# Maxima's steps as one sequence over all units, four or eight steps ahead

## The chip, the cores and the metric

The kernel runs on one core of a Trainium2 chip. The metric is device time in microseconds (us), the median of three runs: 1900.68 us, between 1898.97 and 1903.65. One further execution was profiled; its own time was 1904.93 us, and the profile's span, from the first to the last of the program's own instructions, is 1903.1 us.

Names of engines: TensorE (PE in the profile; PEld are its weight loads), VectorE (DVE), ScalarE (ACT), GpSimd (POOL) and SyncE (SP), which here issues DMAs only. All engines work through their own list of instructions in the order in which the kernel wrote them, and wait for each other by semaphores.

## The reference

The reference has four layers over x, 2048 tokens of 256 features in float32:

```python
x = x + attn_a(layernorm(x))   # 16 query heads, 4 key heads, head size 16, rotary, biases, causal
x = x + ffn(layernorm(x))      # gate and up 256 -> 2048, tanh-gelu, down 2048 -> 256, 4-bit weights
x = x + attn_b(layernorm(x))   # 16 query heads, 16 key heads, causal
x = x + ffn(layernorm(x))      # the same weights
```

In both attentions a row of probabilities is the softmax of q·k/4 over all earlier keys, and the result is the sum of values weighted by it. Only the two attentions are touched by the change.

## The kernel before

**Tiling.** The tokens are cut into four blocks b of 512, and the heads into four groups g of four. One pass of `Attention.run` (L837) goes through 16 units (b, g) in order; the kernel makes two passes, one for each attention. For a unit, softmax is computed in two sweeps over the causal triangle.

The first sweep finds each query's maximum. `scores(i, c, p)` (L651) takes 128 queries i, one block of keys c and one pair of heads p: two matmuls (L658) into a PSUM buffer `ps_s` with queries on partitions, and one VectorE reduce over the keys (L670) into `mx`. A unit of block b has 8(b+1) such steps. On the diagonal block of keys (c equal to b) only the first 128(i+1) keys are computed, and a causal mask is added by eight small matmuls (L633) before the reduce. `gather` (L679) reduces `mx` over the blocks of keys and splits the negated maximum into three bf16 parts, in five small VectorE operations (L682 to L692) that write `m_pad`. `turn` (L696) turns `m_pad` by four matmuls (L699) so that queries stand along the free dimension, and ScalarE copies the result to `mT` (L705).

The second sweep computes the weighted values. `pair(kt, p)` (L739) takes 128 keys kt and a pair of heads p: two matmuls with `sel` put the negated maxima from `mT` into a `ps_s` buffer (L747), two add the scores, this time with keys on partitions (L752), a diagonal pair gets its mask (L633), and ScalarE takes the exponential into `e` (L764). `values` (L718) multiplies `e` by the values into `ps_av` (L732), one block of keys behind the pairs. A unit has 8(b+1) pairs. `end` (L775) does the last values and copies `ps_av` to `o` on ScalarE (L779); `divide` (L782), which runs early in the following unit, turns `o` (L786) and divides by the sums on VectorE (L791, L794).

**What sets the order.** Everything is written out by hand, one step after another, for all engines. `weave(main, side, rest=2)` (L42) puts side steps between main steps in even shares, so that the side steps are used up two main steps before the end. `blend(a, b)` (L60) merges two lists in proportion. In a unit the main steps are its pairs and values. The side steps are the divide of the unit before, and a blend of the maxima's steps of the following unit with other work: preparation of the next block (projections, rotary, the round trip of q and k through DRAM: L426 to L620), output projection of the block before (L806), and in the first pass the unpacking of the feed-forward weights (L307). After the weave come the turn of the following unit's maxima, and then `end`. The very first unit's maxima and turn stand outside of the loop (L978, L994).

**Masks that are owed.** The mask of a diagonal pair or score is not issued at once: it is put on the list `owed`, and the next step calls `settle` (L638) to issue it with the exponential or the reduce behind it. Pairs, values and `gather` settle everything. A score settles only where a score's mask is owed.

**Buffers.** PSUM holds three `ps_s` of two banks each, used in rotation by pairs and scores, one `ps_av` and one `ps_m`. The turn uses `ps_m`, as do divide, preparation and output projection. `qT` has three buffers: at the start of unit n, `load_q` (L610) issues eight DMAs on SP for unit n+2. `mT` and `mx` have two buffers, `m_pad` one.

Of the kernel before, what the change touches and what calls it, by code (L numbers as in the profile page):

```python
# [26 lines left out]
NG = NH // 4  # L27
# [14 lines left out]
def weave(main, side, rest=0):  # L42


    done = 0
    for n, step in enumerate(main):
        first, *second = step if isinstance(step, tuple) else (step,)
        first()
        want = min(len(side), -(-(n + 1) * len(side) // max(1, len(main) - rest)))
        while done < want:  # L50
            side[done]()
            done += 1
        for f in second:
            f()
    while done < len(side):
        side[done]()
        done += 1


def blend(a, b):  # L60

    keyed = [((n + 0.5) / len(a), 0, n, f) for n, f in enumerate(a)]
    keyed += [((n + 0.5) / len(b), 1, n, f) for n, f in enumerate(b)]
    return [f for *_, f in sorted(keyed, key=lambda k: k[:3])]
# [3 lines left out]
def tile_hybrid_layers(  # L68
# [40 lines left out]
    def ps_s():  # L109
        return psum.tile([P, 2, 512], F32, tag="s", name="ps_s", bufs=3)  # L110
# [4 lines left out]
    def ps_m():  # L115
        return psum.tile([P, 512], F32, tag="m", name="ps_m")
# [36 lines left out]
    for src, at in ((bq, 0), (bk, D), (bv, D + 64)):  # L153
        n = src.shape[1]
# [240 lines left out]
    class Attention:  # L395
# [11 lines left out]
        def __init__(self, first, wqkv):  # L407
            self.first, self.wqkv = first, wqkv
            self.kvh = NKV if first else NH
            self.npair = NKV if first else NH // 2  # L410
            self.krows = self.kvh * HD
            self.kT, self.vv, self.qT, self.mT, self.att = {}, {}, {}, {}, {}
            self.q_d, self.k_d = {}, {}
            self.owed = []

        def place(self, pool, b):

# [220 lines left out]
        def settle(self, kind=None):  # L638


            due = [f for k, f in self.owed if kind in (None, k)]
            if due:
                due, self.owed = self.owed, []
                for _, f in due:
                    f()

        def max_steps(self, b, g):

            held = {}

            def scores(i, c, p):  # L651
                if not held:
                    held["mx"] = self.wk.tile([P, NT, 4, NB], F32, tag="mx", name="mx")
                w = TB if c < b else (i + 1) * P
                self.settle("max")
                pt = ps_s()
                for r in range(2):
                    nc.tensor.matmul(  # L658
                        pt[:, r, :w],
                        lhsT=self.qT[b, g][64 * r : 64 * r + 64, p, i * P : (i + 1) * P],  # L660
                        rhs=self.key_rows(c, g, p, r, slice(0, w)),
                        start=True, stop=(c < b),
                    )

                def masked():
                    self.add_mask(pt, 0, w - P)
                    reduced()

                def reduced():
                    nc.vector.tensor_reduce(  # L670
                        held["mx"][:, i, 2 * p : 2 * p + 2, c], pt[:, :, :w], AX.X, ALU.max
                    )

                if c == b:
                    self.owed.append(("max", masked))
                else:
                    reduced()

            def gather():  # L679
                self.settle()  # L680
                nm = self.wk.tile([P, NT, 4], F32, tag="nm", name="nm")
                nc.vector.tensor_reduce(  # L682
                    nm, held["mx"][:, :, :, : b + 1], AX.X, ALU.max, negate=True
                )

                to = m_pad[:, :, :, :6].rearrange("q t r (p s) -> q t p r s", s=3)
                rest = nm.rearrange("q t (p r) -> q t p r", r=2)
                nc.vector.tensor_copy(to[:, :, :, :, 0], rest)
                less = self.wk.tile([P, NT, 2, 2], F32, tag="rest", name="rest")
                nc.vector.tensor_tensor(less, rest, to[:, :, :, :, 0], ALU.subtract)  # L690
                nc.vector.tensor_copy(to[:, :, :, :, 1], less)
                nc.vector.tensor_tensor(  # L692
                    to[:, :, :, :, 2], less, to[:, :, :, :, 1], ALU.subtract
                )

            def turn():  # L696
                pt = ps_m()
                for i in range(NT):
                    nc.tensor.matmul(  # L699
                        pt[:, i * P : (i + 1) * P],  # L700
                        lhsT=m_pad[:, i].rearrange("p r c -> p (r c)"), rhs=ident_b,
                        start=True, stop=True,
                    )
                self.mT[b, g] = self.wk.tile([P, TB], BF16, tag="mT", name="mT")
                nc.scalar.copy(self.mT[b, g], pt)  # L705

            steps = [
                lambda i=i, c=c, p=p: scores(i, c, p)
                for i in range(NT) for c in range(b + 1) for p in range(2)
            ]  # L710
            return steps + [gather], turn
# [125 lines left out]
        def run(self, extra, beside):  # L837


            units = [(b, g) for b in range(NB) for g in range(NG)]  # L840
            per_unit = -(-len(extra) // (len(units) - NG))
            late, ahead = [], []
            for n, (b, g) in enumerate(units):
                more = []
                if g == 0 and b > 0:
                    more += self.out_steps(b - 1)
                if g == 0 and b + 1 < NB:
                    ahead = self.prep_steps(b + 1)
                    few = -(-len(ahead) // 2)
                if n >= NG:  # L850
                    more, extra = more + extra[:per_unit], extra[per_unit:]
                if g < 2:
                    more, ahead = more + ahead[:few], ahead[few:]
                if n + 2 < len(units):
                    self.load_q(*units[n + 2])
                steps, turn = [], None
                if n + 1 < len(units):
                    steps, turn = self.max_steps(*units[n + 1])
                else:
                    more += beside  # L860
                side = late + (blend(steps, more) if steps else more)
                steps, end, divide = self.value_steps(b, g)
                weave(steps, side, rest=2)
                if turn:
                    turn()
                end()
                late = [divide]
            return late + [lambda: None] * 2 + self.out_steps(NB - 1)
# [93 lines left out]
    with tc.tile_pool(name="wk1", bufs=2) as wk, tc.tile_pool(name="kv1", bufs=1) as kv:  # L962
        at.wk = at.qpool = wk
        with tc.tile_pool(name="init", bufs=1) as pool:
# [13 lines left out]
            steps, turn = at.max_steps(0, 0)  # L978
# [6 lines left out]
    with tc.tile_pool(name="kv20", bufs=1, reuse_waits="tile") as kv0, tc.tile_pool(  # L985
# [8 lines left out]
        steps, turn = at.max_steps(0, 0)  # L994
# [60 lines left out]
```

## Time and profile before

| what | value |
|---|---|
| median of three runs | 1900.68 us |
| profiled execution, its own time | 1904.93 us |
| span of the profile | 1903.1 us |
| TensorE busy | 1772.5 us, 93% |
| VectorE busy | 1121.3 us, 59% |
| ScalarE busy | 812.9 us, 43% |
| GpSimd busy | 239.0 us, 13% |
| first pass of attention, units | 51 to 651 us |
| second pass of attention, units | 1011 to 1558 us |

A group of instructions is told in one row: source line, engine, operation, what it writes and reads, how often; then after the first bar its busy time in us and the mean of one in ns; after the second bar the idle time of the engine just before these instructions, and who ended that idle time. Matmuls are pipelined and their ends are modelled, so a busy TensorE is not TensorE at its peak. A row of the timeline has the start in us from the span's start, the length in us, the engine, the line and what is done; in brackets the idle time of that engine before it and who ended it. In the busy time by stretch, the columns are the stretch, its length, and for each engine its busy time and the count of instructions; then the granted clock of TensorE, the DMA engines' share and what they moved.

### The profile page before, as it was taken

To read this page: it belongs to the slowest core of one execution; us is meant where nothing else is said; L and a number is where in the kernel's file an instruction comes from. 1 tells how busy PE (TensorE), PEld (TensorE's weight loads), DVE (VectorE), ACT (ScalarE), POOL (GpSimd) and SP (SyncE) were. 2 spreads that over 40 slices of the span, in tenths; PEclk is the share of its full clock that TensorE was granted. 3 is DMA by queue.
4 is the path that set the end of the run, shared out by engine and by line. 5 is a ranking of instruction groups with operands and counts; after the bars stand their busy time and mean duration, and the time that the engine had idled before them with its cause. 6 is when DMAs were issued, how large, how long until landed. Compare 5 with 4: busy or idle time off the path is not lost. (4 is left out here: it accounts for less than half of the span.)

```text
span 1903.1 us, 31836 instructions
## 1 busy us (share of the span) xinstructions
PE 1772.5 (93%) x13452; PEld 930.8 (49%) x13452; DVE 1121.3 (59%) x1676; ACT 812.9 (43%) x1069; POOL 239.0 (13%) x437
## 2 busy tenths in 40 slices
PE   5788889998999999999998899999899999999999
PEld 3344444344444446566555444444444444756656
DVE  4466587678788153535345667767877715363442
ACT  1334345465666631312223455555566663131221
POOL 4211311310010010111212010010000001011110
PEclk8879899999999999999999899999999999999999
DMA  4511310310101100000403241050000010000000
GB/s 105 118 46 34 73 26 26 72 41 24 34 24 35 45 6 1 0 1 20 102 1 80 56 83 41 12 95 19 23 7 7 2 46 1 11 1 11 7 6 12
DMA packets 42271, 64.24 MB, mean 34 GB/s; under 512 B 13840, under 2 KB 20880, under 8 KB 41872
## 3 DMA queue, kind: packets, MB, share of 16 engines
q1 hardware_dynamic: 33488, 45.93, 8.3%
q0 software_dynamic: 7680, 15.74, 5.0%
q8 instruction: 106, 1.74, 0.4%
q10 hardware_dynamic: 960, 0.52, 0.1%
q14 instruction: 37, 0.30, 0.1%
HBM read 44.24 MB, written 17.83 MB: 33 GB/s over the span
## 5 line engine op out<-in xcount | busy, mean ns | idle before, releaser
L764 ACT ACTIVATE e<-ps_s 128x1024 f32<-128x1024 f32 (+3 forms) x640 | 573.4, 897 | 433.7 <-PE ps_s L752 216.5
L670 DVE TENSOR_REDUCE mx<-ps_s 128x2 f32<-128x1024 f32 (+3 forms) x640 | 656.8, 1060 | 160.9 <-PE ps_s L633 93.2
L732 PE MATMUL ps_av<-e,v 128*32 128x256 f32 (+1 forms) x4608 | 370.6, 386 | 0.7 <-ACT e L764 0.7
L752 PE MATMUL ps_s<-qT,kT 64*128 64x512 f32 (+3 forms) x1280 | 341.9, 527 | 0.0
L658 PE MATMUL ps_s<-kT,qT 64*128 64x512 f32 (+3 forms) x1280 | 268.6, 428 | 45.4 <-DVE mx L670 20.1
L747 PE MATMUL ps_s<-mT,sel 64*128 64x512 bf16 (+3 forms) x1280 | 232.6, 357 | 36.7 <-DVE mx L670 21.4
L915 PE MATMUL ps_s<-xnT,wg 128*128 128x512 f32 x512 | 240.8, 593 | 0.0
L915 PE MATMUL ps_s<-xnT,wu 128*128 128x512 f32 x512 | 240.6, 592 | 0.0
L747 PEld LDWEIGHTS <-sel 64*128 64x128 bf16 x1280 | 77.1, 93 | 275.8 <-issue 269.4
L658 PEld LDWEIGHTS ps_s<-kT,qT 64*128 64x128 f32 x1280 | 125.7, 191 | 150.9 <-ACT e L764 66.9
L923 DVE TENSOR_TENSOR t<-ps_s,t 128x512 f32<-128x512 f32 x128 | 88.1, 689 | 166.4 <-POOL t L922 164.5
L921 ACT ACTIVATE t<-ps_s 128x512 f32<-128x512 f32 x128 | 76.2, 596 | 246.7 <-PE ps_s L915 246.3
L924 ACT ACTIVATE t<-t 128x512 f32<-128x512 f32 x128 | 80.6, 629 | 201.0 <-DVE t L923 201.0
L915 PEld LDWEIGHTS ps_s<-xnT,wu 128*128 128x128 f32 x512 | 97.3, 190 | 122.5 <-issue 122.5
L922 POOL TENSOR_SCALAR t<-t 128x512 f32<-128x512 f32 x128 | 79.3, 620 | 571.1 <-ACT t L921 570.6
L732 PEld LDWEIGHTS ps_av<-e,v 128*32 128x32 f32 x4608 | 97.0, 109 | 102.8 <-issue 79.8
L915 PEld LDWEIGHTS ps_s<-xnT,wg 128*128 128x128 f32 x512 | 95.3, 190 | 105.2 <-issue 103.5
L925 DVE SCALAR_TENSOR_TENSOR t<-t,ps_s 128x512 f32<-128x512 f32 x128 | 88.0, 688 | 89.0 <-ACT t L924 89.0
L752 PEld LDWEIGHTS ps_s<-qT,kT 64*128 64x128 f32 x1280 | 130.4, 198 | 0.0
L940 PE MATMUL ps_m<-wd,inter 128*128 128x256 f32 x512 | 114.5, 380 | 0.0
L940 PE MATMUL ps_av<-wd,inter 128*128 128x256 f32 x512 | 114.5, 380 | 0.0
L633 PE MATMUL ps_s<-mask_t,mask_w 64*128 64x64 bf16 x2048 | 108.4, 199 | 0.0
(125 smaller groups left out, 1171.5 us busy)
## 6 DMA issues: line engine op xcount, KB each, us to landing
qT<-h SPq DMA_DIRECT2D x256, 64.0 KB, 2.2
kT<-h POOLq DMA_DIRECT2D x96, 128.0 KB, 5.7
h<-high SPq DMA_DIRECT2D x24, 256.0 KB, 3.3
h<-low SPq DMA_DIRECT2D x24, 256.0 KB, 3.0
wd<-wd_kept SPq DMA_DIRECT2D x2, 2048.0 KB, 7.8
wd_kept<-dq_d SPq DMA_DIRECT2D x4, 512.0 KB, 2.7
out<-x SPq DMA_DIRECT2D x16, 128.0 KB, 1.7
x<-x SPq DMA_DIRECT2D x3, 512.0 KB, 5.2
```

What stands on the lines that cost most here:

```text
L633: nc.tensor.matmul(pt[:, r, to], lhsT=mask_w[rows, kind, part, :], rhs=mask_t[rows, kind, part, :], start=False, stop=(part == 1),)
L658: nc.tensor.matmul(pt[:, r, :w], lhsT=self.qT[b, g][64 * r : 64 * r + 64, p, i * P : (i + 1) * P], rhs=self.key_rows(c, g, p, r, slice(0, w)),
L670: nc.vector.tensor_reduce(held["mx"][:, i, 2 * p : 2 * p + 2, c], pt[:, :, :w], AX.X, ALU.max)
L732: nc.tensor.matmul(held["av"][32 * j : 32 * j + 32, own], lhsT=self.vv[kt // NT][:, kt % NT, h * VW : h * VW + 32], rhs=es_[j // 2][:, j % ...
L747: nc.tensor.matmul(pt[:, r, q0:], lhsT=sel[64 * r : 64 * r + 64, p, :], rhs=self.mT[b, g][64 * r : 64 * r + 64, q0:], start=True, stop=False,)
L752: nc.tensor.matmul(pt[:, r, q0:], lhsT=self.key_rows(kt // NT, g, p, r, keys), rhs=self.qT[b, g][64 * r : 64 * r + 64, p, q0:], start=Fals ...
L764: nc.scalar.activation(e[:, :, q0:], pt[:, :, q0:], AF.Exp, scale=QK_SCALE)
L915: nc.tensor.matmul(pt[:, k, :], lhsT=w[:, c, fc * P : (fc + 1) * P], rhs=self.xnT[b][:, c, :], start=(c == 0), stop=(c == 1),)
L923: nc.vector.tensor_tensor(t, gate, t, ALU.mult)
L924: nc.scalar.activation(t, t, AF.Tanh, scale=GELU_C)
L925: nc.vector.scalar_tensor_tensor(t, t, 1.0, gate, ALU.add, ALU.mult)
L940: nc.tensor.matmul(po[:, :D], lhsT=inter[:, fc, i * P : (i + 1) * P], rhs=wd[:, fc, :], start=(fc == 0), stop=(fc == NFC - 1),)
```

## The change

Before, a unit carries exactly the maxima's steps of the following unit, and the turn stands at its end. After, the maxima's steps of all units form one sequence, and a unit carries what is left of the following unit's steps and the first four of the unit after that; in the third unit of a block, the first eight (which belong to the next block). The first unit of a pass takes none ahead. The turn is put into this sequence two early steps after the gather, it takes a `ps_s` buffer in place of `ps_m`, and settles what is owed first. In the last unit but one the turn follows the gather after one empty step. `settle` counts scores in a row: the first after another step behaves as before, and from the second on everything owed is settled. The scores, pairs, values, reduces, exponentials and DMAs are the same in number and shape.

```diff
@@ settle
-            due = [f for k, f in self.owed if kind in (None, k)]
-            if due:
+            self.row = self.row + 1 if kind else 0
+            if self.row != 1 or kind in [k for k, _ in self.owed]:
                 due, self.owed = self.owed, []
                 for _, f in due:
                     f()
@@ max_steps
             def turn():
-                pt = ps_m()
+                self.settle()
+                pt = ps_s()[:, 0, :]
                 for i in range(NT):
                     nc.tensor.matmul(
@@ run
             late, ahead = [], []
+
+            due, turn = self.max_steps(*units[1])
             for n, (b, g) in enumerate(units):
...
                 if n + 2 < len(units):
                     self.load_q(*units[n + 2])
-                steps, turn = [], None
-                if n + 1 < len(units):
-                    steps, turn = self.max_steps(*units[n + 1])
+                steps = due
+                if n + 2 < len(units):
+                    coming, next_turn = self.max_steps(*units[n + 2])
+                    early = 0 if n == 0 else 8 if g == NG - 2 else 4
+                    steps, due = due + coming[:early], coming[early:]
+                    steps.insert(len(steps) - max(early - 2, 0), turn)
+                    turn = next_turn
+                elif n + 1 < len(units):
+                    steps, due = due + [lambda: None, turn], []
                 else:
                     more += beside
                 side = late + (blend(steps, more) if steps else more)
                 steps, end, divide = self.value_steps(b, g)
                 weave(steps, side, rest=2)
-                if turn:
-                    turn()
                 end()
                 late = [divide]
```

More of the change, by code (lines that the diff above doesn't have):

```diff
@@ L413, in __init__ @@
             self.q_d, self.k_d = {}, {}
-            self.owed = []
+            self.owed, self.row = [], 0
         def place(self, pool, b):
```

## The prediction

> **What bounds the kernel.** I read the page's busy times first (TensorE 93%, VectorE 59%), then TensorE's groups for what ended its idle time, then busy time unit by unit (a unit is one block of 512 queries and one group of four heads), then the timeline across a unit's end. TensorE's groups that the change touches:
>
> ```profile
> L658 PE MATMUL ps_s<-kT,qT 64*128 64x512 f32 (+3 forms) x1280 | 268.6, 428 | 45.4 <-DVE mx L670 20.1 <-ACT e L764 12.9 <-DMA qT<-h 10.2
> L747 PE MATMUL ps_s<-mT,sel 64*128 64x512 bf16 (+3 forms) x1280 | 232.6, 357 | 36.7 <-DVE mx L670 21.4 <-ACT mT L705 4.8 <-ACT e L764 4.4
> L699 PE MATMUL ps_m<-ident_b,m_pad 128*128 128x128 bf16 x128 | 13.3, 229 | 11.0 <-DVE m_pad L692 8.9 <-DVE low L541 1.6 <-DVE x L946 0.5
> ```
>
> The last columns are TensorE's idle time ahead of the group and its releasers. The turn (L699) waits 11.0 us in all, the pairs behind it 4.8 us for mT, and scores and pairs 41.5 us for VectorE's reduces, which hold the ring of three ps_s buffers.
>
> Busy time by unit in the first pass: units (0,2), (0,3), (2,2), (2,3), (3,1):
>
> ```profile
> core 0: us, PE busy (x) PEld busy (x) DVE busy (x) ACT busy (x) POOL busy (x), PEclk, DMA share, GB/s
> 104.70:117.80 13.10, 11.55 (x171) 6.35 (x171) 7.86 (x15) 6.88 (x11) 0.00 (x0) 0.96 0.14 42
> 117.80:141.10 23.30, 20.25 (x188) 10.72 (x187) 17.25 (x23) 6.58 (x11) 0.00 (x0) 0.63 0.07 23
> 385.80:421.20 35.40, 33.87 (x394) 16.03 (x395) 28.83 (x39) 23.08 (x27) 4.43 (x9) 1.00 0.09 30
> 421.20:464.90 43.70, 37.46 (x411) 17.38 (x411) 37.63 (x47) 23.26 (x27) 4.63 (x9) 1.00 0.10 28
> 517.10:564.30 47.20, 45.41 (x508) 20.51 (x508) 38.55 (x47) 31.35 (x35) 4.58 (x9) 1.00 0.13 41
> ```
>
> A block's fourth unit computes the next block's maxima, eight scores more than its pairs. There VectorE is as busy as TensorE (37.6 against 37.5 of 43.7 us), and TensorE idles 6.2 us; in the third unit it idles 1.5. Unit (3,1) has 96% TensorE: it is bound by TensorE.
>
> The timeline from the end of (3,1) into (3,2), where the turn waits for nothing, and one row from the end of (1,3), where it does:
>
> ```profile
> 563.00 0.23 PE L633 MATMUL ps_s<-mask_t,mask_w 64*128 64x64 bf16 x4
> 563.17 0.40 PE L699 MATMUL ps_m<-ident_b,m_pad 128*128 128x128 bf16 x4
> 563.34 0.38 ACT L764 ACTIVATE e<-ps_s 128x256 f32<-128x256 f32 x1 [0.54 <-PE ps_s L633]
> 563.50 0.69 PE L732 MATMUL ps_av<-e,v 128*32 128x128 f32 x8
> 563.62 0.58 ACT L705 CAST mT<-ps_m 128x512 bf16<-128x512 f32 x1
> 564.23 0.59 ACT L779 COPY o<-ps_av 128x512 f32<-128x512 f32 x1
> 564.25 0.39 PE L747 MATMUL ps_s<-mT,sel 64*128 64x512 bf16 x2
> 564.87 0.65 PE L786 MATMUL ps_m<-ident,o 128*128 128x128 f32 x4
> 565.57 0.26 DVE L791 RECIPROCAL rec<-ps_m 128x16 f32<-128x16 f32 x1 [2.46 <-PE ps_m L786]
> 567.47 0.39 PE L747 MATMUL ps_s<-mT,sel 64*128 64x512 bf16 x2 [0.82 <-DVE mx L670]
> ...
> 285.88 0.40 PE L699 MATMUL ps_m<-ident_b,m_pad 128*128 128x128 bf16 x4 [0.98 <-DVE m_pad L692]
> ```
>
> The turn stands in the shadow of another chain: the last exponential ends at 563.72, the values that need it follow, then o (564.82), the divide's transposes (564.87), rec and att, the first reduce, and the third pair's wait of 0.82 us. The turn and mT fit beside that.
>
> **What the Trainium skill says.** "TensorE: Matmul & The Clock Gate", section Step-by-step, keeps matmuls in program order and lets only weight loads go ahead. The trace agrees: ready values stood 0.98 us behind the turn at 285.88. Its Part 1 says that TensorE's clock is throttled by default and released by activity; (0,3), the unit with the longest VectorE waits for its size, shows a granted clock of 0.63. "PSUM — Partial Sum Buffer", Specifications, gives eight banks of 2 KiB: three ps_s of two banks, av and m fill them, so the turn's new buffer must come out of that ring; no run shows the count of banks. "Perfetto Trace Analysis", section Identifying the Most-Contended Engine, warns that busy matmuls are no measure of headroom; I use idle time before matmuls instead.
>
> **The change, part by part.** The sum is against the profiled execution (span 1903.1, its own time 1904.93 us); the difference is carried to the median of the three runs, 1900.68.
>
> 1. The turn leaves the unit's end. Thirty turns in the two loops move. Followed one by one in the timeline, eleven of them waited: 0.26, 0.59, 0.98, 0.87, 1.16, 0.25, 1.03, 0.44, 0.38, 0.38, 0.64, sum 7.0 us; the rest of the 11.0 stands before the loops. Values, o and divide all come that much earlier: -7.0. The wait for mT behind them (4.8, of which 1.35 at the two starts, so 3.5) I credit with nothing: a pair that starts 0.2 us sooner then waits for o, which in the rows above is ready at 564.82 either way. Bounds 0 and -3.5.
>
> 2. The turn enters the stream. From its first matmul to the next instruction is 563.17 to 563.50: 0.33 us, so far under the last exponential. Thirty of them are 9.9 us; where TensorE waits anyway they vanish. I count the 16 in units over about 92% TensorE (blocks 2 and 3, and most of block 1 in the second pass): +5.3. Bounds 0 and +9.9. If the idle time of the others went as well, the full 9.9 would be due.
>
> 3. Will the turn wait inside the stream? Its gather is five VectorE operations from 561.93 to 563.11, 1.2 us, after a last reduce of 1.2: 2.4 us. Between stand two early scores and two or three pairs, about 0.45 and 1.0 us each with values besides: 2.9 or more. Covered in a regular unit; where a reduce is queued ahead (1.2) it is short by up to 0.7. The turn also takes a ps_s buffer until ACT has copied mT (0.58, behind at most one exponential of 1.03), and the third allocation after it waits for that; two pairs or scores cover it. The early scores queue behind the gather on VectorE, and the pair that wants their buffer waits. No row shows this; bounds 0 and 0.7 x 30 = 21. I take +1.5, as if two or three crowded turns in each pass waited 0.3 to 0.7.
>
> 4. Steps are levelled. From the order: the third and fourth units of blocks 0, 1, 2 go from 8+16, 16+24, 24+32 scores to 12+12, 20+20, 28+28. TensorE's idle time (length less busy) is 1.55, 4.35, 1.5, 1.36, 1.48, 1.6 in the six thirds, sum 11.8, and 3.05, 5.33, 6.24, 5.27, 4.57, 4.46 in the six fourths, sum 28.9. Less the turn waits of item 1 that fall there (1.1 and 3.9) this leaves 10.7 and 25.0. If fourths became like thirds, 14.3 would be gained; but (2,2) gets about 3.2 us more VectorE work on 28.8 (six wide reduces of 1.2 and two narrow of 0.4 for four wide) and so loses most of its slack. I take a third, -5. Bounds -14 and +4 (thirds losing more than fourths gain). The second unit of block 0 gains four narrow scores, and the last unit but one of a pass loses four: the work is the same, and the first has slack (VectorE 43%): 0.
>
> 5. Two scores in a row now settle an owed mask before the second, so that exponential starts one score (0.43 us) earlier. Scores and pairs wait 17.3 us for exponentials; I take -1.5, bounds 0 and -4.
>
> 6. Transfers: the SP order is unchanged, no DMA is added, but q is read a unit earlier. The load for (1,0) landed at 108.7, four us into (0,2), and at 1057.6, 5.5 us in, in the second pass; the first early score stands behind three pairs and four scores, about 6 us in. The keys landed at 91.4 and 1053.1. Hidden; without that cover a stall of 1 to 2 us.
>
> Sum: -7.0 + 5.3 + 1.5 - 5 - 1.5 = -6.7. Profiled 1898.2; median 1894.0.
>
> **Rivals.** *Nothing measurable* (change within 0.3%, 5.7 us, about what a measurement of this kernel can tell from none): the turn was free under the last exponential and now costs its 9.9 in full, and the thirds wait as much as the fourths did. -7.0 + 9.9 + 1.5 - 5 = about 1900. For it: both units of a pair end near 84% VectorE. Against: units of blocks 0 and 1 have TensorE idle time to absorb turns.
>
> *Slower*: the turn stalls the ps_s ring. Place: the pair or score that follows it, held by the gather on VectorE or mT on ACT. At 0.7 us each 30 turns cost 21 instead of 1.5: -6.7 + 19.5 = +13, 1914. The sign turns at 6.7/30 = 0.22 us more for each turn, and 0.3% is passed at 0.41. For it: ring waits are already the largest (41.5 us). Against: two pairs lie between gather and turn.
>
> *Much faster*: the fourths do become like thirds, -14, and turns vanish in idle time: -7 + 2 - 14 - 3 = about 1879. For it: (0,3) at clock 0.63 would regain speed. Against: VectorE's total is unchanged.
>
> **How the numbers follow.** Gain of some 4 to 16 us: 0.43, its own range 1885 to 1896; much faster 0.08; nothing measurable 0.31; slower 0.18. A sliver of the first case falls inside 0.3%. Faster 0.49, same 0.33, slower 0.18. The range reaches halfway into the slower case and to the edge of the much faster: 1882 to 1909.
>
> **What would show it.** Right: the turn's idle time falls from 11.0 to about 4 to 6, fourths near 39 us and thirds near 38 in block 2. Wrong: L747 and L658 waiting longer for mx, or the turn waiting for m_pad inside the stream; (3,1) longer by over 0.5 us; the pair's two units summing to 79 or more in block 2.

## The result: slower by 0.92%

The changed kernel takes 1918.18 us, the median of four runs (1916.03 to 1919.72), against 1899.83 us of the kernel before (four runs, 1898.87 to 1903.65). The ratio is 1.0092, with a 95% interval from 1.0075 to 1.0110. The profiled execution took 1919.72 us, its span is 1917.9 us, 14.8 us more than before. The time lies outside of the forecast range, near the 1914 of the rival that was called *slower* and was given 0.18.

TensorE's groups of the changed kernel, which answer to those of before (line, engine, operation, what it writes and reads, count; busy us and mean ns; idle time before it and who ended it). The line numbers moved by one: 748 was 747, 700 was 699, 733 was 732, 787 was 786.

```profile
L733 PE MATMUL ps_av<-e,v 128*32 128x256 f32 (+1 forms) x4608 | 380.2, 387 | 6.0 <-ACT e L765 6.0
L658 PE MATMUL ps_s<-kT,qT 64*128 64x512 f32 (+3 forms) x1280 | 275.7, 431 | 45.5 <-DVE mx L670 21.6 <-DMA qT<-h 11.0 <-ACT e L765 10.1
L748 PE MATMUL ps_s<-mT,sel 64*128 64x512 bf16 (+3 forms) x1280 | 232.9, 359 | 31.0 <-DVE mx L670 14.6 <-ACT e L765 10.8 <-ACT mT L706 1.3
L787 PE MATMUL ps_m<-ident,o 128*128 128x128 f32 x128 | 21.3, 290 | 3.7
L700 PE MATMUL ps_s<-ident_b,m_pad 128*128 128x128 bf16 x128 | 12.9, 224 | 14.5 <-DVE m_pad L692 6.9 <-DVE mx L670 5.9 <-ACT e L765 1.7
```

The turn (L700) was to wait less and waits more, 14.5 us in place of 11.0. Its releasers are new: half of the time it now waits for a reduce (5.9) or an exponential (1.7), that is, for a buffer of the ring, and not for its own data. At the units' ends the values (L733) wait 6.0 us for the last exponential, which the turn used to cover. The values' row before was:

```profile
L732 PE MATMUL ps_av<-e,v 128*32 128x256 f32 (+1 forms) x4608 | 370.6, 386 | 0.7 <-ACT e L764 0.7
```

These waits do not add up to the loss. Span less busy time, TensorE was idle for 132.3 us after 130.6, only 1.7 us more; its busy time grew by 13.1 us, from 1772.5 to 1785.6. A part of that is the clock: TensorE ran at half its clock for 82 us of the profiled execution before and for 96 of the changed one, which accounts for 7 us at most, half of the 14. The rest goes with less overlap: the values' group is busy for 9.6 us more at nearly the same mean (387 ns after 386). So the waits tell where the order rubs; the price has to come from runs.

Busy time by unit, the same units of the first pass as before, (0,2), (0,3), (2,2), (2,3), (3,1); the second column is the length, then TensorE, its weight loads and VectorE:

```profile
core 0: us, PE busy (x) PEld busy (x) DVE busy (x) ACT busy (x) POOL busy (x), PEclk, DMA share, GB/s
108.80:129.60 20.80, 16.88 (x180) 8.89 (x180) 12.58 (x19) 6.81 (x10) 0.00 (x0) 0.75 0.09 27
129.60:147.40 17.80, 14.29 (x170) 7.46 (x168) 13.27 (x19) 6.81 (x10) 0.00 (x0) 0.89 0.10 28
393.40:431.40 38.00, 35.54 (x410) 16.93 (x408) 31.80 (x43) 23.09 (x26) 3.11 (x7) 1.00 0.08 25
431.40:471.20 39.80, 36.74 (x395) 16.55 (x394) 34.84 (x43) 23.09 (x26) 5.91 (x12) 1.00 0.14 30
524.00:571.70 47.70, 45.82 (x510) 20.55 (x508) 38.41 (x47) 31.29 (x34) 4.67 (x10) 1.00 0.13 41
```

In block 2 of this pass the levelling looks as forecast: 38.0 and 39.8 us where I had written 38 and 39, together 77.8 after 79.1. In block 0 it does not: 20.8 and 17.8 after 13.1 and 23.3. Over all six pairs of third and fourth units (each from one copy to `o` to the next) the sum went from 342.3 to 345.7 us. The regular unit (3,1) grew by half a microsecond.

The end of (3,1) in the timeline of the changed kernel (start, length, what; in brackets the idle time before it):

```profile
570.54 0.23 PE L633 MATMUL ps_s<-mask_t,mask_w 64*128 64x64 bf16 x4
570.70 0.41 PE L733 MATMUL ps_av<-e,v 128*32 128x128 f32 x4
570.87 0.38 ACT L765 ACTIVATE e<-ps_s 128x256 f32<-128x256 f32 x1 [0.54 <-PE ps_s L633]
571.31 0.41 PE L733 MATMUL ps_av<-e,v 128*32 128x128 f32 x4 [0.20 <-ACT e L765]
571.65 0.39 PE L748 MATMUL ps_s<-mT,sel 64*128 64x512 bf16 x2
571.77 0.59 ACT L780 COPY o<-ps_av 128x512 f32<-128x512 f32 x1 [0.51 <-PE ps_av L733]
572.41 0.66 PE L787 MATMUL ps_m<-ident,o 128*128 128x128 f32 x4
573.10 0.26 DVE L792 RECIPROCAL rec<-ps_m 128x16 f32<-128x16 f32 x1 [2.98 <-PE ps_m L787]
```

From the last mask to the divide's transposes it is 570.54 to 572.41, 1.87 us; before it was 563.00 to 564.87, 1.87 us. Taking the turn out of a quiet end gained nothing, as the prediction's first step said. But VectorE now idles 2.98 us before the reciprocal in place of 2.46: the gather, five VectorE operations, has left the end of the unit, and nothing has taken its place.

That last number is worth adding up. The reciprocal's group, in the kernel before and then in the changed one, shows VectorE's idle time at the units' ends:

```profile
L791 DVE RECIPROCAL rec<-ps_m 128x16 f32<-128x16 f32 x32 | 8.2, 257 | 86.6 <-PE ps_m L786 86.6
```

```profile
L792 DVE RECIPROCAL rec<-ps_m 128x16 f32<-128x16 f32 x32 | 8.2, 257 | 106.2 <-PE ps_m L787 106.2
```

It is 19.6 us more. VectorE is not the busiest engine, and its idle time is not itself the loss: e1 below has 100.4 us of it and is faster than the kernel before. But it shows unused room. The weave keeps the last two pairs of every unit free of side steps, which made room for gather and turn; the changed kernel keeps them free although neither stands there any more, and puts more steps between the remaining pairs.

And this is the middle of (0,2) in the second pass, where the turn now stands:

```profile
1068.34 0.23 DVE L692 TENSOR_TENSOR m_pad<-rest,m_pad 128x16 bf16<-128x16 f32 x1
1068.43 2.35 DVE L670 TENSOR_REDUCE mx<-ps_s 128x2 f32<-128x1024 f32 x2
1069.14 0.81 ACT L765 ACTIVATE e<-ps_s 128x768 f32<-128x768 f32 x1 [1.54 <-PE ps_s L633]
1069.70 0.38 PE L700 MATMUL ps_s<-ident_b,m_pad 128*128 128x128 bf16 x4 [0.66 <-DVE mx L670]
1070.12 0.59 ACT L706 CAST mT<-ps_s 128x512 bf16<-128x512 f32 x1 [0.17 <-PE ps_s L700]
1070.84 0.50 PE L658 MATMUL ps_s<-kT,qT 64*128 64x128 f32 x2 [0.75 <-DVE mx L670]
```

The turn's data are ready at 1068.57, yet it starts at 1069.70: it waits for the first of two reduces to give a ps_s buffer back. The score behind it waits for the second. TensorE stands idle for 1.4 us around one turn; by the order of the buffers, a score in the turn's place would have waited for the first reduce too, so the turn's own share is less.

### The profile page after: what moved, and what is told of

The parts are those of the page before. It is cut to its first block, busy times and chain, and to the rows that moved or that the text cites. A ratio compares the mean times of both kernels' runs of the same rounds, so it can differ in the third digit from the quotient of the medians.

```text
span 1917.9 us, 31840 instructions
## 1 busy us (share of the span) xinstructions
PE 1785.6 (93%) x13452; PEld 935.6 (49%) x13452; DVE 1120.5 (58%) x1676; ACT 813.5 (42%) x1069; POOL 238.9 (12%) x437
## 5 line engine op out<-in xcount | busy, mean ns | idle before, releaser
L733 PE MATMUL ps_av<-e,v 128*32 128x256 f32 (+1 forms) x4608 | 380.2, 387 | 6.0 <-ACT e L765 6.0
L658 PE MATMUL ps_s<-kT,qT 64*128 64x512 f32 (+3 forms) x1280 | 275.7, 431 | 45.5 <-DVE mx L670 21.6
L748 PE MATMUL ps_s<-mT,sel 64*128 64x512 bf16 (+3 forms) x1280 | 232.9, 359 | 31.0 <-DVE mx L670 14.6
L748 PEld LDWEIGHTS <-sel 64*128 64x128 bf16 x1280 | 71.9, 93 | 270.0 <-issue 265.6
L658 PEld LDWEIGHTS ps_s<-kT,qT 64*128 64x128 f32 x1280 | 130.9, 192 | 147.5 <-DVE mx L670 56.6
L733 PEld LDWEIGHTS ps_av<-e,v 128*32 128x32 f32 x4608 | 99.0, 109 | 112.9 <-issue 79.0
L633 PE MATMUL ps_s<-mask_t,mask_w 64*128 64x64 bf16 x2048 | 115.0, 200 | 0.0
```

The costliest lines, as they stand in the source:

```text
L633: nc.tensor.matmul(pt[:, r, to], lhsT=mask_w[rows, kind, part, :], rhs=mask_t[rows, kind, part, :], start=False, stop=(part == 1),)
L658: nc.tensor.matmul(pt[:, r, :w], lhsT=self.qT[b, g][64 * r : 64 * r + 64, p, i * P : (i + 1) * P], rhs=self.key_rows(c, g, p, r, slice(0, w)),
L733: nc.tensor.matmul(held["av"][32 * j : 32 * j + 32, own], lhsT=self.vv[kt // NT][:, kt % NT, h * VW : h * VW + 32], rhs=es_[j // 2][:, j % ...
L748: nc.tensor.matmul(pt[:, r, q0:], lhsT=sel[64 * r : 64 * r + 64, p, :], rhs=self.mT[b, g][64 * r : 64 * r + 64, q0:], start=True, stop=False,)
```

## Experiments

Two theories stood at the start. Theory 1: the turn's place in the stream costs. Theory 2: the steps ahead cost. A third, that the new settling rule costs, came with e4. Each run was made beside the kernel before on the same chip; ratios are to that kernel, their 95% intervals stand in brackets, and I compare ratios between runs. One per cent is 19 us. The granted clock differs between the kernels, which the medians and ratios do not tell; the part on the clock below compares at the same clock.

**e1, the turn back at the unit's end, steps ahead kept.**

```diff
@@ turn
-                self.settle()
-                pt = ps_s()[:, 0, :]
+                pt = ps_m()
@@ run
-                    steps.insert(len(steps) - max(early - 2, 0), turn)
-                    turn = next_turn
...
                 weave(steps, side, rest=2)
+                if turn:
+                    turn()
+                turn = next_turn
                 end()
```

> The changed kernel (1918.2) with the turn put back behind the weave and into ps_m; the steps still run four or eight ahead. Theory 1, the turn's place costs: inside the stream it takes 0.33 us of TensorE each and waits 11.0 us in all, at the end it lies under the last exponential and its gather is long done. Then 10 + 11 us go and the 6.6 us gained at the units' ends stay: about 1897, turn waits under 1 us inside the loops. Theory 2, the steps ahead cost (third and fourth units of block 0 took 7.8 us more than before, the first two 5.5): 1912 to 1918. If both: between, about 1905.

Measured: 1896.23 us against 1902.36, ratio 0.9973 [0.9961, 0.9986]. Theory 1 said 1897. Moving the turn, with its buffer, took the kernel from 0.9% slower to 0.3% faster; the difference of the ratios is 0.0119, some 22 us. The turn's row shows its waits nearly gone (5.2 us, of which about 4 before the loops):

```profile
L699 PE MATMUL ps_m<-ident_b,m_pad 128*128 128x128 bf16 x128 | 13.4, 231 | 5.2 <-DVE m_pad L692 3.5 <-DVE low L541 1.2 <-DVE x L954 0.5
```

So the steps ahead did remove waits before the turn (11.0 to 5.2, 5.8 us), about as much as e1 gains (6.1 us). That these are the same microseconds is argued from the sums and not shown; the settling rule may have a share in them (e14). For the levelling of third and fourth units, for which I had booked 5 us more, no clear sum is left.

**e2, the turn in the stream, no steps ahead.**

```diff
-                    early = 0 if n == 0 else 8 if g == NG - 2 else 4
-                    steps, due = due + coming[:early], coming[early:]
-                    steps.insert(len(steps) - max(early - 2, 0), turn)
+                    steps, due = due + [lambda: None, turn], coming
```

> No steps ahead; the turn in the stream and in ps_s, one empty step behind its gather; the settling of the changed kernel. Theory 1 (the turn's place costs): 10 us of issue, waits as before the change or more since gather and turn are only one or two pairs apart, 1908 to 1916. Theory 2 (the steps ahead cost): 1895 to 1902, third and fourth units as before the change.

Measured: 1937.86 us, ratio 1.0189 [1.0171, 1.0207]. Both expectations were too low; the direction is that of theory 1. The turn waits 23.9 us, all for m_pad, and VectorE's idle time before the reciprocal is 156.4 us. The steps ahead are what makes a turn in the stream bearable: without them gather and turn must be done before the last two pairs, and the scores before those. Since the gather moved too, e2 doesn't price the turn's place by itself.

**e4, the former settling rule in the changed kernel, and e10, the new rule alone in the kernel before.**

```diff
-            self.row = self.row + 1 if kind else 0
-            if self.row != 1 or kind in [k for k, _ in self.owed]:
+            due = [f for k, f in self.owed if kind in (None, k)]
+            if due:
```

> The changed kernel with the former settling rule (a score settles only an owed score's mask). Theories 1 and 2: 1918 within 2 us, up to 1.5 us slower since the exponentials start up to one score later. Theory 3, the new rule costs (the mask put between two scores holds back the second score's reduce): 1906 to 1912.

> The kernel before with the new settling rule alone; turn, buffers and order of steps as before. In the changed order the rule saved 5.9 us (e4). If the 5 us by which e1 beats the kernel before come from the rule: 1895 to 1898 against 1901. If they come from the steps ahead: 1900 to 1902.

Measured: e4 1924.16 us, ratio 1.0111 [1.0094, 1.0129]; e10 1901.89 against 1903.09, ratio 0.9994 [0.9982, 1.0007]. Theory 3 falls. The rule is worth nothing measurable in the order before and some 4 us in the changed order (0.0019 in ratio, the intervals overlap).

**e14, steps ahead and turn at the end with the former rule** (the edits of e1 and e4 together).

> The kernel of e1 with the former settling rule: steps ahead alone. The rule alone was worth 1 us (e10), but 5.9 us in the changed order (e4). If steps ahead are a gain of their own: 1895 to 1900 against 1902 to 1903 before. If they need the rule, because two scores in a row are then more often followed by a waiting pair: 1901 to 1905.

Measured: 1899.84 against 1903.30, ratio 0.9989 [0.9976, 1.0002]. It lies at the upper edge of the first expectation, but the interval holds 1, so a gain of the steps ahead alone isn't shown. Some 3 us of e1's gain seem to go with the rule.

**e5, no steps ahead in block 0.**

```diff
-                    early = 0 if n == 0 else 8 if g == NG - 2 else 4
-                    steps, due = due + coming[:early], coming[early:]
+                    early = 0 if b == 0 else 8 if g == NG - 2 else 4
+                    steps, due = due + (coming[:early] or [lambda: None]), coming[early:]
```

> The changed kernel, but no steps ahead in the four units of block 0 (the turn there one empty step behind its gather); from block 1 on as changed. Theory 2 in its narrow form (the loss is the steps ahead in block 0, whose short units have no room): the 13.3 us that block 0 took more than before in both passes go, less the turn's own cost there, so 1907 to 1910. Theory 1: 1914 to 1918, since the turn still stands in the stream.

Measured: 1926.54, ratio 1.0120 [1.0101, 1.0139]: no faster than the changed kernel, whose interval it overlaps. Theory 2 in its narrow form, which said 1907 to 1910, falls too; block 0 looked worst by unit, but leaving out its steps ahead brought nothing.

**What in the turn's place costs: e7, e8, e9.** All three are e1 with a filler at the places where the changed kernel has its turn. The work is added, and nobody needs it.

```diff
+        def filler(self):            # e7
+            self.settle()
+            pt = ps_s()[:, 0, :]
+            for i in range(NT):
+                nc.tensor.matmul(
+                    pt[:, i * P : (i + 1) * P], lhsT=ident_b, rhs=ident_b,
+                    start=True, stop=True,
+                )
+            nc.scalar.copy(self.wk.tile([P, TB], BF16, tag="fill", name="fill"), pt)
...
+            pt = ps_s()[:, 0, :8]    # e8, in place of the matmuls and the copy above
+            nc.tensor.matmul(pt, lhsT=ident_b, rhs=ident_b[:, :8], start=True, stop=True)
+            nc.scalar.copy(self.wk.tile([P, 8], BF16, tag="fill", name="fill"), pt)
...
+            self.settle()            # e9: the next pair issues the four matmuls
+            self.extra = True        # into its own buffer, ahead of its own
```

> The kernel of e1 (turn at the unit's end, steps ahead; 1896.2) with a filler at the places in the stream where the changed kernel has its turn: it settles, takes a ps_s buffer, four matmuls of the turn's size from a constant, and a ScalarE copy of 512 columns that nobody reads (added work, 31 times). It never waits for m_pad. If the turn's cost in the stream is its room on TensorE and in the ring of ps_s: 1911 to 1917, most of the 22 us between e1 and the changed kernel. If it is the wait for the gather on VectorE: 1897 to 1902.

> As e7, but the filler is one matmul and one copy of 8 columns: it takes the ps_s buffer, and next to no time on TensorE or ScalarE. If the ring is what costs (each pair or score after it has one buffer less between it and the reduce or exponential it waits for): 1905 or more, at least half of e7's cost. If issue costs: 1897 to 1900.

> As e7, but the four matmuls go into the next pair's own ps_s buffer ahead of its own, with no buffer and no copy of their own: room on TensorE alone. If issue costs: 0.33 us x 31 = 10 us, 1904 to 1907. If TensorE had room there: 1896 to 1899.

Measured: e7 1915.36, ratio 1.0065 [1.0051, 1.0080]; e8 1920.04, ratio 1.0086 [1.0072, 1.0100]; e9 1897.11, ratio 0.9970 [0.9961, 0.9979]. Against e1 these are +17, +21 and about 0 us. A buffer of the ring with next to no work in it costs about as much as the whole turn. The turn's four matmuls without a buffer cost nothing in the medians, but that is not the same as nothing: all 22 executions of e9 had a higher granted clock (0.983 to 0.992) than nearly all of e1 (0.971 to 0.985), and at the same clock e9 is some 8 us longer, as shown below. The wait for m_pad isn't needed for the loss, since fillers have no data to wait for. The filler's own row, in e8 and then in e9, shows the wait for the ring at its first matmul:

```profile
L716 PE MATMUL ps_s<-ident_b 128*128 128x8 bf16 x30 | 5.2, 174 | 7.1 <-DVE mx L670 5.2 <-ACT e L770 1.9
```

```profile
L750 PE MATMUL ps_s<-ident_b 128*128 128x128 bf16 x120 | 11.8, 220 | 1.9 <-DVE mx L670 1.3 <-ACT e L774 0.5
```

The releasers of e8's row (5.2 from mx, 1.9 from e) are those of the changed kernel's turn, with nearly the same sums (5.9 and 1.7).

**e13, the turn at the unit's end, but in the ring** (e1 with `ps_s` in place of `ps_m` in the turn).

> The kernel of e1 (1896.2), with the turn at the unit's end in a ps_s buffer instead of ps_m. If a fourth user of the ring costs wherever it stands: 1906 or more. If only in the midst of scores and pairs, since at the end two pairs stand without scores and the ring is slack: 1896 to 1900.

Measured: 1896.18 against 1903.30, ratio 0.9961 [0.9941, 0.9980]. The same further user of the ring costs nothing measurable where the pairs stand without scores.

**e11, the turn at the end in block 0 alone.**

```diff
-                    steps.insert(len(steps) - max(early - 2, 0), turn)
-                    turn = next_turn
+                    if b > 0:
+                        steps.insert(len(steps) - max(early - 2, 0), turn)
+                    at_end, turn = turn if b == 0 else None, next_turn
...
+                if at_end:
+                    at_end(apart=True)     # the turn in ps_m
```

> The changed kernel (1918.2), but in the four units of block 0 the turn stands at the unit's end in ps_m; in the other blocks it stays in the stream and in the ring. If the ring costs evenly, 8 of 31 turns leave it: a quarter of the 22 us, 1911 to 1914. If it costs mainly in block 0, whose short units have the fewest pairs between two allocations and fall to half clock (7.1 of the 12.6 us by which the second pass of the changed kernel is longer than e1's): 1902 to 1907.

Measured: 1919.67, ratio 1.0074 [1.0056, 1.0093]. That is 0.0018 under the changed kernel (the intervals overlap), no more than an even share for 8 of 31 turns. The cost does not sit mainly in block 0.

**e16, the filler of e8 with no reader** (its copy is left out), and **e19, the changed kernel with the copy to mT on VectorE.**

```diff
-            nc.scalar.copy(self.wk.tile([P, 8], BF16, tag="fill", name="fill"), pt)   # e16
...
-                nc.scalar.copy(self.mT[b, g], pt)                                     # e19
+                nc.vector.tensor_copy(self.mT[b, g], pt)
```

> As e8 (1920.0 against 1896.2 of e1), but nobody reads the filler's 8 columns: the buffer is free again as soon as its one matmul is done, and only the rotation of the three buffers is moved on by one. If the rotation costs (the next pair must wait for the step three allocations back, now one step nearer): 1912 or more. If it is the hold until ScalarE comes to the copy, behind exponentials and the preparation's copies: 1896 to 1903.

> The changed kernel with the copy to mT on VectorE instead of ScalarE. If the turn's buffer is held too long because the copy stands behind exponentials and preparation on ScalarE: 1906 to 1913. If rotation and issue cost, or if VectorE's queue of reduces is no shorter: 1916 to 1924.

Measured: e16 1907.52 against 1901.87, ratio 1.0022 [1.0011, 1.0034]; e19 1926.89, ratio 1.0129 [1.0111, 1.0147]. e16 lies between its two expectations: against e1 it costs 0.0049, 9 us, and e8 0.0113, 21 us. Moving the rotation on by one costs somewhat under half in the medians, and two thirds or more at the same clock (below); the rest goes with the reader, that is, with holding the buffer until ScalarE comes to it or with the small copy itself, which these runs don't tell apart. The hold is not cured by another reader: from the turn's last matmul to the start of the copy it is 0.51 us in the mean on VectorE (e19) and 0.30 on ScalarE (the changed kernel).

**e15 and e17, side steps over all pairs.** e15 is e1, e17 the changed kernel, each with nearly the same edit: e15 keeps the last two pairs free in the last unit of a pass only, e17 in the last two units.

```diff
-                weave(steps, side, rest=2)
+                weave(steps, side, rest=0 if turn else 2)                # e15
+                weave(steps, side, rest=0 if n < len(units) - 2 else 2)  # e17
```

> The kernel of e1, with side steps spread over all pairs of a unit (none of the last two kept free of scores), which the gather, now four steps or more before the end, allows. If VectorE's idle stretch of 2.5 us at each unit's end is what bounds the third and fourth units: 1885 to 1892. If the last reduces then hold up the divide of the next unit, or PE-bound units see no difference: 1895 to 1900.

> The changed kernel (turn in the stream and in the ring) with side steps over all pairs of a unit, as in e15, which with the turn at the end took 1877.5. If the turn's place costs what it costs between e1 and the changed kernel, about 22 us: 1897 to 1902. If the loss is a matter of the free last pairs, which the turn's three empty steps crowd out: 1880 to 1888.

Measured: e15 1877.47 against 1903.30, ratio 0.9860 [0.9837, 0.9883]; e17 1874.62 against 1901.87, ratio 0.9852 [0.9832, 0.9873]. Both beat both kernels by far, and e17 is the changed kernel with one argument altered. With the last pairs in use the medians no longer show the turn's place: what cost 22 us costs nothing. At the one clock that both have, 0.982, e17 took 1881.4 us and e15 1877.5 and 1878.2, so a few us may be left. Both sides moved. e17's turn waits 7.3 us in all in place of 14.5, and e15's turn at the end, whose gather now stands close before it, waits 11.9 us in place of e1's 5.2. The kernel before with its side steps over all pairs was not run, so how much of the gain needs the steps ahead isn't measured. Scores, turn, values and reciprocal of e17:

```profile
L658 PE MATMUL ps_s<-kT,qT 64*128 64x512 f32 (+3 forms) x1280 | 269.2, 419 | 32.5 <-ACT e L765 10.9 <-DMA qT<-h 9.4 <-DVE mx L670 8.6
L700 PE MATMUL ps_s<-ident_b,m_pad 128*128 128x128 bf16 x128 | 12.9, 225 | 7.3 <-DVE m_pad L692 3.5 <-DVE mx L670 2.9 <-ACT e L765 0.8
L733 PE MATMUL ps_av<-e,v 128*32 128x256 f32 (+1 forms) x4608 | 373.9, 382 | 5.4 <-ACT e L765 4.1
L792 DVE RECIPROCAL rec<-ps_m 128x16 f32<-128x16 f32 x32 | 8.2, 257 | 48.1 <-PE ps_m L787 48.1
```

VectorE's idle time at the units' ends falls from 106.2 to 48.1 us, scores wait 8.6 us for reduces in place of 21.6 (pairs, not shown, 17.4 in place of 14.6), and the turn's waits inside the loops are about 4 us.

**A count that goes with the times.** From the order of TensorE's instructions in the traces I counted, between each pair and the next, the steps that take a ps_s buffer (scores, and turn or filler where they use the ring), and summed what exceeds one. Such a step follows another ring step at once, with fewer pairs and values between a buffer's use and its next.

| kernel | steps in excess of one | VectorE idle before the reciprocal, us | ratio to before |
|---|---|---|---|
| e15 | 98 | 47.9 | 0.9860 |
| e17 | 129 | 48.1 | 0.9852 |
| e1 | 150 | 100.4 | 0.9973 |
| before | 160 | 86.6 | 1 |
| e8 | 168 | 106.3 | 1.0086 |
| changed kernel | 169 | 106.2 | 1.0092 |
| e2 | 184 | 156.4 | 1.0189 |

The kernels order themselves alike by all three columns, but for e1 against before, e15 against e17 and the near tie of e8 with the changed kernel. The count is a companion of the time, not its proof: e16, e7, e4, e5 and e19 all have 168 or 169, with ratios from 1.0022 to 1.0129. What is shown is the effect of the single edits.

**The granted clock.** Executions of one kernel differ by their mean granted clock, and the time goes with it: e1 took 1905.6 us at 0.971 and 1890.1 at 0.985, about 1.1 us for each 0.001. So I compared kernels once more in two ways. The middle columns take all executions of a kernel that had the clock named, and give their median, with their number in brackets. The last column takes blocks 1 to 3 of the second pass in the profiled executions, eleven turns or fillers, where TensorE had its full clock almost throughout (at half clock for 0.7 us in e16, not at all in the other rows), and gives the difference in length to e1.

| kernel | clock | median, us | e1 at that clock | difference | blocks 1 to 3, to e1 |
|---|---|---|---|---|---|
| before | 0.978, 0.979 | 1906.1 (21) | 1896.0 (3) | +10.1 | +5.2 |
| changed kernel | 0.978, 0.979 | 1918.1 (3) | 1896.0 (3) | +22.1 | +5.5 |
| e7, matmuls, buffer and copy | 0.978, 0.979 | 1916.0 (3) | 1896.0 (3) | +20.0 | +5.5 |
| e8, buffer and small copy | 0.974 to 0.976 | 1918.5 (3) | 1902.9 (4) | +15.6 | +4.7 |
| e16, buffer with no reader | 0.978, 0.979 | 1908.6 (9) | 1896.0 (3) | +12.6 | +3.1 |
| e9, matmuls alone | 0.984, 0.985 | 1897.8 (3) | 1889.9 (2) | +7.9 | +3.3 |

Most cells hold few executions, but the two columns agree. The four matmuls do cost, 0.3 us a place, and a higher clock hid it in e9's medians; why e9 has that clock isn't shown. If the fillers themselves bring it, their net price is nothing, as the medians say. The buffer with its reader (e8) costs more than the matmuls alone, and all of it together (e7) costs less than the sum of both. The changed kernel is slower than the kernel before at the same clock too, by some 12 us. Yet in blocks 1 to 3 of the second pass, at full clock, the two are equally fast: in the traces its 14.8 us arise up to the end of the first unit of each pass and in block 0. e5 and e11 say that neither leaving out the steps ahead there nor moving the turns there brings more than an even share of them back.

**What stays open.** TensorE ran at half its clock for 82 us of the profiled execution before, 96 of the changed one, 99 of e1, 114 of e8, 41 of e9 and 51 of e17. Ring waits and half clock may feed each other: the comparison at the same clock takes the clock out, but it does not tell which of the two comes first.

## Why the prediction was wrong

The sign was wrong, and the step that failed is step 3, the wait inside the stream and the place in the ring, which I took at +1.5 us. A buffer of the ring taken at the turn's places, with next to no work in it, cost 21 us in the medians and 16 at the same clock (e8). The term of step 4 did not come either, but it could not have turned the sign.

1. *The turn leaves the end*, -7.0: right. Unit by unit, from the last mask to the divide's transposes, the chain shortened by 6.6 us in sum, and by nothing in the quiet ends. The bracket for the wait for mT, credited with nothing, was right too: the next pair starts 1.12 us after the last mask in place of 1.25, and the divide still at 1.87. e1 keeps most of it, 5.5 us.
2. *The turn's own 0.33 us*, +5.3 with bounds 0 and 9.9: sized rightly for each turn, 0.3 in blocks 1 to 3 of the second pass (e9 against e1). Alone, over all places, it is about 8 us at the same clock, near the upper bound. Beside the ring it adds little: e7 is some 4 us over e8 at the same clock.
3. *The ring*, +1.5 with bounds 0 and 21: 16 to 21 in e8, the upper end. I had worked out that two pairs lie between gather and turn, and that this covers the gather. That is true where steps run ahead. In the first unit of a pass none do, so the turn stands right behind its gather; 2.9 of the 3.4 us that turns inside the loops wait for m_pad are there (1.15 at 68.3 and 1.73 at 1032.6). I had then said that two pairs or scores cover the hold of the buffer. That is the error, and a second wait was in no term: the turn itself waits for a buffer, 7.6 us in all. The turn is a third kind of ring user in a stretch where pairs and scores already waited 41.5 us for the same three buffers. The rival named the place (the step that follows, held in the ring) and the price, 0.7 us a turn; it blamed the gather on VectorE or the copy to mT on ScalarE. e8 and e16 show the rotation and the reader; a gather is not needed for it.
4. *Levelling*, -5: about nothing by itself. In the first pass block 2 fell as computed, in the second it didn't (76.5 us after 76.4), and block 0 took it back. I looked at the scores per unit and not at where in the unit they may stand. The two free pairs at the end were kept, though the gather's work had left them. e15 and e17 show what lay there: 20 to 45 us in the medians (not split between levelling and the free pairs).
5. *Settling*, -1.5: within what was measured, 0 to -4.
6. *Transfers*, 0: right; scores waited 11.0 us for q, after 10.2.

At the same clock, terms 1, 4 and 5 together are e1 against the kernel before, -10, and terms 2 and 3 the changed kernel against e1, +22: in sum +12. The traces have +14.8, with 0.975 after 0.978 for the clock, and the medians +18. The rival's 1914 came near, with the right place and half of the right reason.

The Trainium skill, "TensorE: Matmul & The Clock Gate", section Step-by-step, keeps matmuls in program order, and the ring's price rests on it: a turn, score or pair that waits for its buffer holds back everything behind it, as the 1.4 us at 1069.70 show.

## What to carry to other kernels

A step that is moved into a stream has two prices, its time on the engine and its place in the buffers' rotation. Measure each with a filler, one that takes a buffer and does nothing and one that does the work without a buffer; here the buffer with its reader cost more, and both together cost less than the sum. Compare such runs at the same granted clock, or in stretches at full clock: equal medians hid 8 us of added work in e9. When work leaves a reserved stretch (here the two pairs kept free for gather and turn), give the stretch back in the same edit: here that was worth 20 us with the turn at the end (e15) and 43 with the turn in the stream (e17), and moving steps and turn without it was worth 6 at best (e1).

## What the runs showed of the hardware that was not expected

One matmul of 8 columns and one copy of 8 columns, 30 times, lengthened a kernel of 1896 us by 21 us, 0.7 us each, because of the PSUM buffers that they took; at the same granted clock it was 16 us. Four matmuls of 128 columns at the same places without buffers of their own changed the median by less than 1 us, yet at the same clock they cost some 8: their 22 executions ran at 0.983 to 0.992, those of the kernel without them at 0.971 to 0.985. Eight matmuls of the values took 0.69 us in one stretch (563.50, before) and 0.41 us for each half when a wait split them (570.70 and 571.31, after).
